# Patches of layer 2: the next exponential ahead of the root's steps, a function table loaded ahead of the first square, and one constant copied by ScalarE

## The chip, the cores and the metric

The kernel runs on one core of a Trainium2 chip. The time is device time in microseconds (us) of one execution. Ten executions of the kernel before took between 6381.21 and 6408.22 us, with a median of 6394.25 us. One more execution was taken with the hardware profiler: it took 6396.54 us, and its span, from its first to its last instruction, is 6394.8 us. All durations below are from that execution, and all times inside it are counted from the start of its span.

The engines of the core are called TensorE (PE in the profile, with PEld for its loads of weights), VectorE (DVE), ScalarE (ACT), GpSimd (POOL) and SyncE (SP, which here only issues transfers). Each engine works through its own list of instructions in order, and an instruction that waits holds up all that stand behind it on that engine.

## The reference: what is computed

The input is x of shape (4, 192, 64, 64): four images of 192 channels. Four layers follow one another: layer 0 (a deformable convolution, channel attention and an MLP), layer 1 (attention of all 4096 positions with all others), layer 2 (attention in overlapping windows, then a gate and an MLP) and layer 3 (a small convolution whose weights come from the mean of the image). The change lies in the attention of layer 2, and in one constant. What matters of the reference:

```python
y = _conv1x1(_ln_c(x, n1g, n1b), qkv_w, qkv_b)       # layer norm over channels, then q, k, v
cols = _unfold(y, WS, STRIDE, PAD)                   # 8x8 windows, 6 apart: 11 x 11 of them
...
attn = jnp.einsum('blhic,blhjc->blhij', q, k)
attn = attn + bias[None, None]
e = jnp.exp(attn - jnp.max(attn, axis=-1, keepdims=True))
s = jnp.sum(e, axis=-1, keepdims=True)
s_img = _reverse(s, H, W)                            # overlapping windows are added up
o = jnp.einsum('blhij,blhjc->blhic', e, v)
o_img = _reverse(o, H, W).reshape(B, HEADS, ch, H, W)
out = (o_img / s_img[:, :, None]).reshape(B, C, H, W)
```

`_ln_c` subtracts the mean over the channels and multiplies with `rsqrt(var + 1e-05)`.

## The kernel before, in words

The kernel takes the images one after the other. For each image b the layers run mostly one behind the other, and the attention of layer 2, here called the patches, is the function `windows(b, ...)` (line 1060). Most of the program is ordered by a scheduler. The main part of `windows` stands in a block `with tc.manual_schedule()` (line 1311): there the instructions of each engine keep the order in which the code issues them.

**The rows of windows.** The image has 11 rows of windows, `wr` = 0 to 10, with 11 windows each. A row is worked on in three groups `g` of four windows (three in the last group), and a group in two pairs. For one group:

- `scores(wr, g)`: TensorE multiplies q and k (line 1185) into the PSUM tile `s`, of which there is one; VectorE adds the bias (line 1191) and so makes the tile `ex`.
- `lowered` takes off the maximum (VectorE, lines 1201 and 1202), and ScalarE then takes the exponential of `ex` in place (line 1333 for the first group, 1368 for all others). It covers 128x768 elements.
- `summed` adds up the exponentials (VectorE, lines 1207 and 1211).
- `turned(wr, g, pair)`: TensorE computes v (line 1228) and transposes the exponentials (line 1236); ScalarE copies both out of PSUM (lines 1233 `vs`, and 1240 `et`).
- `outputs` multiplies them (TensorE, lines 1256 and 1264) for the pair before the one that was just turned.

The tiles of `v`, `t`, `qk` and `rb` share one PSUM tag `a` with two buffers, so that each of these products on TensorE needs the reader of the last but one to have ended.

The exponential is issued one group ahead: in group g the code issues the scores of the next group first, then both pairs of its own group, and at the end, behind the pairs, the exponential of the next group.

**The layer norm of later rows** is cut into steps (`norm_steps`, line 1107) that `links` advances up to a named point. For row wr + 2 the square (ScalarE, line 1112) is issued in group 0 of row wr, the sums over channels (TensorE, `variances`, line 383) and the inverse root at the end of group 1 (`norm(wr + 2, INVERSE)`, line 1365), and the spreading over partitions (TensorE, line 392, `pb`) in group 2. The steps of the root, called the root's steps here, are: a square of the mean (ScalarE, line 400), two operations of VectorE (lines 401 and 402), and then on ScalarE a logarithm (line 363) and an exponential (line 364). They stand ahead of the next group's exponential of line 1368.

**The sums of a row** are inverted in group 1 of the row after it, between its two pairs: `inverses` (line 1289) issues a logarithm (line 1295) and an exponential (line 1296) on ScalarE. In group 2, `finish` (line 1298) spreads them with TensorE (line 1301, `rb`), and VectorE multiplies (line 1302).

**The function tables.** ScalarE evaluates Ln, Exp, Gelu and others from a table set that must be loaded before; a load is an instruction of its own on ScalarE (`ACT_TABLE_LOAD` in the profile). The kernel issues some loads by hand with `table`; where an activation is not served by the set that the program's builder takes to be loaded, the builder puts a load right in front of it, and this load then carries the activation's line number.

```python
    def table(name):
        if in_order and in_order[0] != name:
            in_order[0] = name
            if name == GELU:
                nc.scalar.preload_act_table(AF.Gelu)        # line 356
            else:
                nc.scalar.preload_act_table_set(name)       # line 358

    def inverse_root(r, pv):
        table(LN_EXP)
        nc.scalar.activation(r, pv, AF.Ln, bias=eps)        # line 363
        nc.scalar.activation(r, r, AF.Exp, scale=-0.5)      # line 364
```

`LN_EXP` is the set that has both Ln and Exp. The list `in_order` remembers the set that was loaded last by hand; it is non-empty only inside the blocks with a manual order. In the patches it is appended, and `table(LN_EXP)` called, right behind the square of row 0 and two warming products; later calls from `inverse_root` find the name unchanged and issue nothing.

**Warming.** `keep_warm(p, n)` (line 748) issues n products of TensorE whose result nobody reads, to fill its idle time. At the head of the patches they write the tile `warm`.

**The constant.** `constants` (line 181) is a generator that prepares weights during layer 0 of the first image. One of its steps collects biases in the tile `wide` (128x46) from PSUM (lines 239 to 255), with a copy on VectorE at the end.

Of the kernel before, what the change touches and what calls it, by code (L numbers as in the profile page):

```python
# [12 lines left out]
AF = mybir.ActivationFunctionType  # L13
# [20 lines left out]
LN_EXP, GELU = "natural_log_exp_and_others", "gelu"  # L34
# [22 lines left out]
NWIN = 11  # L57
# [24 lines left out]
def conv_seq_kernel(ctx: ExitStack, tc: tile.TileContext, a, out: bass.AP):  # L82
    nc = tc.nc

    def pool_of(**kw):

        return tc.tile_pool(**({} if kw.get("space") == DRAM else {"reuse_waits": "tile"}), **kw)
# [7 lines left out]
    def const(shape, name):  # L95
        return wpool.tile(shape, F32, tag=name, name=name)
# [89 lines left out]
    def constants():  # L186
# [53 lines left out]
        with pool_of(name="wideps", bufs=1, space=PSUM) as pp:  # L240
            n = sum(n for name, n in _V96 if name in _WIDE)
            wide = const([M, 2, n], "wide")
            p = pp.tile([M, 2, n], F32, tag="p", name="p_wide")
            at = 0
            for name, n in _V96:
                if name in _WIDE:
                    cols = slice(at, at + n)
                    at += n
                    for to, of, k in (
                        (p[0:P, 0, cols], slice(0, P), 0), (p[P:M, 0, cols], slice(0, M - P), 1),  # L250
                        (p[0:Q, 1, cols], slice(M - P, P), 1), (p[Q:M, 1, cols], slice(M - P, P), 1),
                    ):
                        nc.tensor.matmul(to, lhsT=ident[:P, of], rhs=V[name][:, k, :], start=True, stop=True)
                    VW[name] = wide[:, :, cols]
            nc.vector.tensor_copy(wide, p)
        yield
        fc1_dram, fc1_bias = folded("fc1", V["l0_g2"], V["l0_b2"], V["l0_bfc1"])
        yield
# [2 lines left out]
        with pool_of(name="foldq", bufs=1, space=PSUM) as pp:  # L261
            p = pp.tile([128, 2, 512], F32, tag="p", name="p_qkv")
# [15 lines left out]
        with pool_of(name="outb", bufs=1, space=PSUM) as pp:  # L278
            p = pp.tile([P, 2], F32, tag="outb", name="pob")
# [69 lines left out]
    in_order = []  # L349
# [6 lines that stand above are left out]
                nc.scalar.preload_act_table(AF.Gelu)  # L356
            else:
                nc.scalar.preload_act_table_set(name)
# [76 lines left out]
    def links(steps, upto=None):  # L435

        while True:
            try:
                link = next(steps)
                if upto is not None and link == upto:  # L440
                    return None
            except StopIteration as end:
                return end.value
# [304 lines left out]
    def keep_warm(p, n):  # L748

        m, width = p.shape  # L750
        columns = spread.rearrange("p j n -> p (j n)")[:, 0:width]
        for _ in range(n):
            nc.tensor.matmul(p, lhsT=ident[:, 0:m], rhs=columns, start=True, stop=True)
# [306 lines left out]
    def windows(b, oi, load_image):  # L1060
# [3 lines left out]
        with ExitStack() as s:  # L1064
# [6 lines left out]
            def new_rows(wr):  # L1071

                top = STRIDE * wr - PAD
                r0, r1 = (PAD if wr == 0 else WS - STRIDE), min(WS, H - top)
                return r0, r1, top + r0
# [31 lines left out]
            def norm_steps(wr, src, dst, rows):  # L1107

                n, name = src.shape[2], f"l2n1_{b}_{wr}"
                q = n // 4  # L1110
                sq = s1.tile([P, 2, 512], F32, tag="ln_sq", name=f"sq_{name}", bufs=2)[:, :, :n]
                nc.scalar.activation(sq, src, AF.Square)
                yield SQUARE
                pv = ps.tile([128, 512], F32, tag="n", name=f"pv_{name}")
                variances(pv[:, 0:q], src, mean192)
                variances(pv[:, 128 : 128 + q], sq, mean192)
                r = s1.tile([128, 128], F32, tag="ln_r", name=f"r_{name}", bufs=2)[:, 0:q]
                spread_variance(r, pv[:, 0:q], pv[:, 128 : 128 + q])
                yield from inverse_root_steps(r, r)
                pb = spread_quarters(r, n, P, ps, name).rearrange("p (r c) -> p r c", r=rows)  # L1120
                for k in range(2):
                    nc.vector.tensor_tensor(dst[:, k], src[:, k, :].rearrange("p (r c) -> p r c", r=rows), pb, ALU.mult)

            def norm(wr, upto=None):

                r0, r1, _ = new_rows(wr)
                if wr not in norms:
                    norms[wr] = norm_steps(wr, given.pop(wr), sets[wr % 2][0][:P, :, r0:r1, inside], r1 - r0)
                links(norms[wr], upto)
# [180 lines left out]
            groups = -(-NWIN // WG)  # L1310
            with tc.manual_schedule():
                warm = ps2.tile([128, 512], F32, tag="a", name=f"warm_{b}")[:, 0:384]
                norm(0, SQUARE)
                keep_warm(warm, 2)
                in_order.append(None)
                table(LN_EXP)
                norm(0, VARIANCE)
                keep_warm(warm, 2)
                norm(0)
                keep_warm(warm, 1)  # L1320
                shared(0, 0)
                project_rows(0, 0)
                norm(1, SQUARE)
                project_rows(0, 1)
                norm(1, VARIANCE)
                queries(0)
                inputs(0)
                norm(1)
                shared(1, 0)
                load(2)  # L1330
                ex, top = scores(0, 0)
                lowered(0, 0, ex, top)
                nc.scalar.activation(ex, ex, AF.Exp)
                due = None
                for wr in range(NWIN):
                    for g in range(groups):
                        nxt = (wr, g + 1) if g + 1 < groups else (wr + 1, 0)
                        if 0 < wr < NWIN - 2 and g == 0:
                            norm(wr + 2, SQUARE)
                        if nxt[0] < NWIN:  # L1340
                            sc, top = scores(*nxt)
                        sums = summed(wr, g, ex)
                        if nxt[0] < NWIN:
                            lowered(*nxt, sc, top)
                        if wr + 3 < NWIN and g == 1:
                            load(wr + 3)
                        for pair in range(WG // 2):
                            ops = turned(wr, g, pair, (ex, sums))
                            if due is not None:
                                outputs(*due)  # L1350
                                if g == 0 and pair == 0:
                                    collect(wr - 1)
                            due = ops
                            if g == 0 and wr + 1 < NWIN:
                                project_rows(wr + 1, pair)
                            if wr == 0 and g == 0 and pair == 0:
                                norm(2, SQUARE)
                            if wr > 0 and g == 1 and pair == 0:
                                inverses(wr - 1)
                            if wr > 0 and g == 2:  # L1360
                                finish(wr - 1, pair)
                            if wr + 2 < NWIN and g == 2 and pair == 0:
                                norm(wr + 2)
                        if wr + 2 < NWIN and g == 1:
                            norm(wr + 2, INVERSE)
                        if nxt[0] < NWIN:
                            ex = sc
                            nc.scalar.activation(ex, ex, AF.Exp)
                        if g == 0 and wr + 1 < NWIN:
                            for i in (1, 2):  # L1370
                                shared(wr + 1, i)
                            queries(wr + 1)
                            inputs(wr + 1)
                        if g == 2 and wr + 2 < NWIN:
                            shared(wr + 2, 0)
                    if wr == 1:
                        load_image()
                outputs(*due)
                collect(NWIN - 1)
                inverses(NWIN - 1)  # L1380
                keep_warm(ps2.tile([128, 512], F32, tag="a", name=f"warm2_{b}")[:, 0:384], 4)
                for h in range(2):
                    finish(NWIN - 1, h)
                in_order.pop()
# [611 lines left out]
    with ExitStack() as s:  # L1996
        sb, pool = (s.enter_context(pool_of(name=n, bufs=1)) for n in ("norms0", "l0d0"))
        ps = s.enter_context(pool_of(name="l0dps", bufs=2, space=PSUM))
        wide = s.enter_context(pool_of(name="l0dps2", bufs=5, space=PSUM))
# [119 lines left out]
```

## Time and profile before

| what | value |
|---|---|
| time, median of 10 (lowest, highest) | 6394.25 us (6381.21, 6408.22) |
| time of the profiled execution | 6396.54 us |
| its span | 6394.8 us, 106283 instructions |
| PE / PEld busy | 5921.8 us (93%) / 4052.4 us (63%) |
| DVE / ACT / POOL busy | 4603.1 (72%) / 3778.3 (59%) / 2107.3 us (33%) |
| TensorE's granted clock, mean | 0.961 |
| table loads on ScalarE, all lines | 164, of 1283 ns each |
| the patches of the four images | about 1481 to 1752, 2997 to 3268, 4514 to 4786, 5755 to 6025 us |

A row of busy time sums an engine's instructions. TensorE's products are pipelined and their ends are modelled, so that 93% doesn't mean that it runs at its peak. A line of the timeline gives the start, the time until the end, the engine, the source line, the operation, out<-in, how many instructions were merged, and in brackets how long the engine stood idle just before and who ended that. A line of a stretch (windows) gives start and end, the length, the busy time of each engine with its count of instructions, TensorE's granted clock as a share of full speed, and the share and rate of the DMA engines.

### The profile page before, as it was taken

The numbers are of one execution on the slowest core, as the hardware profiler recorded it, in microseconds if no ns is written. First come the engines' busy times: TensorE is split into PE (matmuls) and PEld (weight loads), VectorE is DVE, ScalarE is ACT, GpSimd is POOL, SyncE is SP. The second block draws the span as 40 slices with busy tenths as digits, with TensorE's granted clock in tenths as the row PEclk, the third lists the DMA queues.
The fourth block names the chain that finished last, engine by engine and source line by source line (L and its number), as shares of the span: only waits on it lengthen the run. The fifth ranks groups of instructions, "written<-read, shape, count | busy, mean of one in ns | idle before, by whom it ended". The sixth has DMA issues, their size and how long they took to land.

```text
span 6394.8 us, 106283 instructions
## 1 busy us (share of the span) xinstructions
PE 5921.8 (93%) x40528; PEld 4052.4 (63%) x40528; DVE 4603.1 (72%) x6850; ACT 3778.3 (59%) x6552; POOL 2107.3 (33%) x2293
## 2 busy tenths in 40 slices
PE   7888999999989899999988899999998989999897
PEld 4555688886644568887654458888654457776543
DVE  3764199985578669996676839998567867765667
ACT  3764388875654358885654438887565436545542
POOL 2763077752200037772210008775220000003200
PEclk8889999999989899999998999999998999999998
DMA  6995267751010266772110057775101020001000
GB/s 191 300 314 159 85 193 224 224 180 37 24 29 16 73 197 218 229 225 72 34 35 25 20 138 229 223 224 171 38 24 29 18 62 11 13 15 36 7 7 22
DMA packets 330116, 698.59 MB, mean 109 GB/s; under 512 B 59894, under 2 KB 216838, under 8 KB 328839
## 3 DMA queue, kind: packets, MB, share of 16 engines
q0 software_dynamic: 92736, 455.22, 21.7%
q1 hardware_dynamic: 236038, 235.78, 13.4%
q8 instruction: 321, 5.26, 0.3%
q14 instruction: 189, 1.54, 0.1%
q10 hardware_dynamic: 832, 0.79, 0.0%
HBM read 611.25 MB, written 78.87 MB: 108 GB/s over the span
## 4 chain that ended last, share of the span: by engine, by line
PE 65%; DVE 18%; ACT 7%; DMA 5%; issue 4%; POOL 1%; SPq 0%; DVEq 0%; ACTq 0%; POOLq 0%
PE y L1041 11%; PE s L973 10%; PE h L650 7%; DMA ring<-table,idx 2%; PE po L538 2%; PE v L1228 2%; DVE ha L1412 2%; PE h L1604 2%; PE qk L1150 2%; PE o L878 2%; PE qk L1151 2%; DVE ga L1412 2%; DVE gate L1412 2%; DVE row L639 1%; PE t L1236 1%
## 5 line engine op out<-in xcount | busy, mean ns | idle before, releaser
L632 POOL DMA_INDIRECT ring<-table,idx x1152 | 1673.5, 1453 | 949.8 <-DMA wkT<-in_wkT_dram 269.8
L973 PE MATMUL s<-ths,ph 96*128 96x256 f32 x4096 | 981.9, 381 | 5.1 <-ACT sc L975 2.8
L973 PEld LDWEIGHTS s<-ths,ph 96*128 96x128 f32 x4096 | 776.4, 191 | 129.0 <-ACT sc L975 4.5
L638 ACT ACTIVATE row<-ring,pos 128x384 f32<-128x384 f32 x1152 | 672.7, 609 | 235.0 <-DVE xo L643 146.1
L639 DVE SCALAR_TENSOR_TENSOR row<-ring,fr,row 128x384 f32<-128x384 f32 x1152 | 675.6, 615 | 109.1 <-ACT row L638 103.7
L1041 PE MATMUL y<-sc,gx 128*97 128x256 f32 x3008 | 716.4, 379 | 0.0
L1041 PEld LDWEIGHTS y<-sc,gx 128*97 128x97 f32 x3008 | 489.3, 164 | 127.6 <-issue 5.1
L642 ACT ACTIVATE xo<-row,pos 128x192 f32<-128x192 f32 x1152 | 486.0, 448 | 70.3 <-PE h L650 33.7
L643 DVE SCALAR_TENSOR_TENSOR xo<-row,fr,xo 128x192 f32<-128x192 f32 x1152 | 446.8, 413 | 38.7 <-ACT xo L642 36.8
L975 ACT COPY sc<-s 128x1024 f32<-128x1024 f32 x376 | 377.4, 1004 | 156.8 <-PE s L973 153.5
L1038 DVE TENSOR_TENSOR sc<-sc,mbs 128x1024 f32<-128x1024 f32 x376 | 453.7, 1219 | 19.9 <-ACT mbs L999 19.9
L1039 ACT ACTIVATE sc<-sc 128x1024 f32<-128x1024 f32 x376 | 393.3, 1053 | 75.1 <-DVE sc L1038 71.9
L980 DVE TENSOR_TENSOR top<-top,sc 128x1024 f32<-128x1024 f32 x282 | 344.5, 1222 | 127.2 <-ACT sc L975 127.0
L650 PE MATMUL h<-ti,xo 128*128 128x192 f32 x2304 | 434.6, 327 | 0.0
L650 PEld LDWEIGHTS h<-ti,xo 128*128 128x128 f32 x2304 | 388.8, 190 | 28.8 <-issue 8.6
L650 PE MATMUL h<-kept,xo 128*128 128x192 f32 x960 | 243.5, 386 | 66.8 <-DVE xo L643 58.9
L1412 DVE SCALAR_TENSOR_TENSOR ga<-gate,v,ga 128x1024 f32<-128x1024 f32 x234 | 300.4, 1284 | 6.7
L1654 POOL COPY gate<-gate 128x192 f32<-128x192 f32 x12 | 4.2, 349 | 903.9 <-ACT gate L1647 903.9
L1191 DVE TENSOR_TENSOR ex<-s,bias 128x768 f32<-128x768 f32 x132 | 126.1, 956 | 242.2 <-PE s L1185 238.7
L650 PEld LDWEIGHTS h<-kept,xo 128*128 128x128 f32 x960 | 173.2, 213 | 160.9 <-DVE xo L643 116.8
L855 PE MATMUL h<-d_l0m,fc 128*128 128x256 f32 x768 | 215.5, 424 | 59.1 <-ACT z L1610 22.5
L1240 ACT COPY et<-t 64x384 f32<-64x384 f32 x484 | 232.0, 479 | 58.1 <-PE t L1236 51.9
(403 smaller groups left out, 11136.6 us busy)
## 6 DMA issues: line engine op xcount, KB each, us to landing
ti<-table SPq DMA_DIRECT2D x768, 48.0 KB
ring<-table,idx POOLq DMA_INDIRECT x1152, 5.1
xnd<-xn SPq DMA_DIRECT2D x4, 3270.0 KB
xi<-in_x_dram SPq DMA_DIRECT2D x32, 384.0 KB
xk<-xd SPq DMA_DIRECT2D x32, 384.0 KB
xd<-xc SPq DMA_DIRECT2D x64, 192.0 KB
table<-tt SPq DMA_DIRECT2D x32, 384.0 KB
xc<-xd SPq DMA_DIRECT2D x60, 192.0 KB
```

Of the source, the lines that this page charges most:

```text
L632: nc.gpsimd.indirect_dma_start(out=gt.rearrange("p q r c -> p (q r c)"), out_offset=None, in_=corners, in_offset=bass.IndirectOffsetOnAxis ...
L638: nc.scalar.activation(row, gt[:, 0], AF.Copy, scale=pos[:, t, 9 + tap : 10 + tap])
L639: nc.vector.scalar_tensor_tensor(row, gt[:, 1], fr[:, t, 9 + tap : 10 + tap], row, ALU.mult, ALU.add)
L642: nc.scalar.activation(xo[:, j, :], row[:, 0, :], AF.Copy, scale=pos[:, t, tap : tap + 1])
L643: nc.vector.scalar_tensor_tensor(xo[:, j, :], row[:, 1, :], fr[:, t, tap : tap + 1], xo[:, j, :], ALU.mult, ALU.add)
L650: nc.tensor.matmul(acc[m // 2][:, bass.ts(m % 2, C)], lhsT=xo.rearrange("p j c -> p (j c)")[:, bass.ts(m, 128)], rhs=tt, start=t == 0 and ...
L973: nc.tensor.matmul(p[:, t, :], lhsT=ph[:, bass.ts(G * g + t, 128)], rhs=ths[i], start=True, stop=True)
L975: nc.scalar.copy(to, p)
L1038: nc.vector.tensor_tensor(ex, ex, mbs[i].unsqueeze(1).to_broadcast([128, G, QN]), ALU.add)
L1039: nc.scalar.activation(ex, ex, AF.Exp)
L1041: nc.tensor.matmul(py, lhsT=gx[:, G * g + t, :], rhs=ex[:, t, :], start=g == 0 and t == 0, stop=g == NG - 1 and t == G - 1,)
L1412: nc.vector.scalar_tensor_tensor(acc[:, b], src(tap, b), w[:, tap : tap + 1], acc[:, b], ALU.mult, ALU.add)
```

## The change

Three edits, in the functions `constants` and `windows`:

1. The copy of the constant `wide` out of PSUM goes from VectorE to ScalarE.
2. At the head of the patches, `in_order.append(None)` and `table(LN_EXP)` move ahead of the square of row 0, and six more warming products are issued between them and the square.
3. Inside the rows, the exponential of the next group moves from the end of the group to its second pair, right behind that pair's `turned` and `outputs`. It so comes ahead of the projections of the next row's second half in group 0, ahead of the root's steps in group 1, and ahead of `finish` in group 2.

```diff
-            nc.vector.tensor_copy(wide, p)
+            nc.scalar.copy(wide, p)
...
                 warm = ps2.tile([128, 512], F32, tag="a", name=f"warm_{b}")[:, 0:384]
+                in_order.append(None)
+                table(LN_EXP)
+                keep_warm(warm, 6)
                 norm(0, SQUARE)
                 keep_warm(warm, 2)
-                in_order.append(None)
-                table(LN_EXP)
                 norm(0, VARIANCE)
...
                             due = ops
+                            if pair == 1 and nxt[0] < NWIN:
+                                ex = sc
+                                nc.scalar.activation(ex, ex, AF.Exp)
                             if g == 0 and wr + 1 < NWIN:
                                 project_rows(wr + 1, pair)
...
                             norm(wr + 2, INVERSE)
-                        if nxt[0] < NWIN:
-                            ex = sc
-                            nc.scalar.activation(ex, ex, AF.Exp)
                         if g == 0 and wr + 1 < NWIN:
```

## The prediction, made before the changed kernel was run

> **What bounds the kernel now.** I read the page first: the span, the busy shares, and the chain that ended last by engine.
>
> ```profile
> span 6394.8 us, 106283 instructions
> PE 5921.8 (93%) x40528; PEld 4052.4 (63%) x40528; DVE 4603.1 (72%) x6850; ACT 3778.3 (59%) x6552; POOL 2107.3 (33%) x2293
> PE 65%; DVE 18%; ACT 7%; DMA 5%; issue 4%; POOL 1%; SPq 0%; DVEq 0%; ACTq 0%; POOLq 0%
> ```
>
> TensorE carries the chain, ScalarE has 7% of it. But the change touches one stage, so the second view is busy time in the stretches of the four patches.
>
> ```profile
> 1481.00:1752.00 271.00, 250.92 (x3776) 165.02 (x3774) 158.78 (x235) 166.46 (x354) 76.58 (x207) 0.97 0.12 30
> sum 1084.00, PE 1001.72 PEld 659.10 DVE 635.32 ACT 665.46 POOL 312.49; mean PE 250.43 PEld 164.78 DVE 158.83 ACT 166.36 POOL 78.12
> ```
>
> 1084 of 6395 us are patches, and ScalarE is busy for 61% of them. That looks like room, so the third view is its timeline around one place: row 6, from group 1 into group 2.
>
> ```profile
> 1629.25 0.97 ACT L1240 COPY et<-t 64x384 f32<-64x384 f32 x2
> 1630.25 0.52 ACT L1295 ACTIVATE rs<-ot 6x384 f32<-6x384 f32 x1
> 1630.80 0.52 ACT L1296 ACTIVATE rs<-rs 6x384 f32<-6x384 f32 x1
> 1631.35 0.32 ACT L1233 COPY vs<-v 128x192 f32<-128x192 f32 x1
> 1631.56 0.97 ACT L1240 COPY et<-t 64x384 f32<-64x384 f32 x2
> 1632.55 0.25 ACT L400 ACTIVATE r_l2n<-pv_l2n 128x96 f32<-128x96 f32 x1
> 1633.38 0.37 ACT L363 ACTIVATE r_l2n<-r_l2n,eps 128x96 f32<-128x96 f32 x1 [0.57 <-DVE r_l2n L402]
> 1633.78 0.28 ACT L364 ACTIVATE r_l2n<-r_l2n 128x96 f32<-128x96 f32 x1
> 1633.97 0.83 ACT L1368 ACTIVATE ex<-ex 128x768 f32<-128x768 f32 x1
> 1634.70 0.30 ACT L1233 COPY vs<-v 128x192 f32<-128x192 f32 x1
> ```
>
> For 5.5 us ScalarE has no gap but the 0.57 us in which VectorE works on the root. TensorE's timeline shows who needs it:
>
> ```profile
> 1634.85 0.55 PE L1236 MATMUL t<-ident,ex 128*128 128x128 f32 x3 [1.24 <-ACT ex L1368]
> 1635.84 0.89 PE L1301 MATMUL rb<-rs,headsel 128*96 128x384 f32 x2
> ```
>
> The transposes wait 1.24 us for the exponential, and `rb` cannot start before `vs` (1635.0) has freed its PSUM buffer. So once a row, of 22.9 us (from the `et` at 1606.3 to that at 1629.25), ScalarE sets the pace, just where its two logarithms and their exponentials stand.
>
> **What the change does to the instructions.** I compared the order of instructions on each engine in the two built kernels. VectorE loses the copy of `wide`, TensorE gains 6 warming products an image, POOL and SyncE keep their order, DMA issues and queues included. On ScalarE the exponentials move as the diff says. But it has 343 table loads instead of 164. The hand-issued load, now first in its block and with no input, is placed at the top of the whole program: eight loads stand there, Ln-and-Exp and Gelu in turn, where one stood. When the patches come, layer 1 has left another set loaded, and the builder puts a load before every Ln and the Exp behind it:
>
> ```
> L1295 load; L1295 Ln; L1296 load; L1296 Exp; ... L363 load; L363 Ln; L364 load; L364 Exp
> ```
>
> These are 44 at each of the four lines, 176 in all; with three more at the top, 179. The list of before can be trusted here: its 164 loads are, line by line, those in the trace (41+37+24+23+20+4+4+4+4+3). The exponentials of 128x768 need none, since an Exp always ran last.
>
> A load costs this:
>
> ```profile
> 12.41 1.28 ACT L372 ACT_TABLE_LOAD   x1 [1.25 <-PE pv_l L383]
> 13.70 0.37 ACT L372 ACTIVATE r_l<-pv_l,eps 128x128 f32<-128x128 f32 x1
> 1769.35 1.28 ACT L372 ACT_TABLE_LOAD   x1
> 1771.06 0.40 ACT L372 ACTIVATE r_l0m<-r_l0m,eps 128x128 f32<-128x128 f32 x1 [0.43 <-DVE r_l0m L402]
> ```
>
> 1.28 us, and the activation starts 0.01 later. The second pair has the form of line 363: the load runs at once and the activation alone waits for VectorE, so the load covers that wait.
>
> Two statements of the Trainium skill are set against these rows. "ScalarE: Activation LUTs", What ACT_TABLE_LOAD costs, adds a drain of about 1380 ns to each switch; the 0.01 us above shows none, and with it 176 loads would cost 243 us more. Its Table sets section says that Ln followed by Exp needs one load, since one set has both; by that the 176 loads would not exist and the time would hardly change. The built order shows them.
>
> **The cost, step by step** (one image).
>
> *Rows 1 to 8.* I replay the timeline above with the new order, durations and steps unchanged. `et` ends at 1630.22; load to 1631.52; Ln to 1632.06; load to 1633.35; Exp to 1633.88; `vs` and `et` of the second pair take 1.18 as before, to 1635.09; now the exponential, to 1635.95 (the next can start at 1635.85); the square of the mean to 1636.12; load, which covers the 0.57, to 1637.4; Ln to 1637.8; load to 1639.1; Exp to 1639.4; `vs` to 1639.7; `rb` at 1639.75, not 1635.84. That is 3.9 us a row. The bounds: 5.13 if none of the four loads were covered, 2.5 if two of them fell into waits. The move itself, which was to take away the 1.24 us, gains nothing at `rb`: `vs` still stands behind the root's steps. In groups 0 and 2 it only fills gaps of ScalarE (0.88 us idle before `qs` at 1625.98). 8 x 3.9 = 31.2.
>
> *Row 0* has no sums to invert: only `pb` waits for the root. The exponential and two loads come ahead of it; 1522.28 becomes about 1523.2: 0.9. *Rows 9 and 10* and the end have no root but the two loads of `inverses`: 2.5 each, 7.5. In row 10 TensorE waits 0.82 us for that chain already, so none is covered.
>
> *The head.* For row 0's norm ScalarE waits 1.16 us for VectorE, which hides most of the first load: 0.15 + 1.28 = 1.4. For row 1's, 0.73 + 1.28 = 2.0: TensorE waits 1.63 us for it today. The old load there (1482.2) lay beside TensorE's work, its removal gains nothing. Of the six warming products two come between the last two products `wy` of layer 1, four behind them and straight ahead of the sums of row 0. One takes 0.78 us (the two behind the sums fill 1487.3 to 1488.9; each is two records). The two between the `wy` run from 1485.3 to 1486.9, partly in the 0.57 for which TensorE waits there now, and put the last `wy` (1486.0) off by 0.9; with the four behind it, 0.9 + 3.1 = 4.0. In the last image the scheduler puts them at the start of layer 1: one where TensorE waits 0.42 for a transfer, four ahead of `th` in an unbroken run of TensorE, one in a wait of 0.56: 0.4 + 3.1 = 3.5.
>
> Sum: 31.2 + 0.9 + 7.5 + 3.4 = 43.0, times four 172; warming 3 x 4.0 + 3.5 = 15.5; together 187.5.
>
> *Top of the program.* Eight loads take 10.3 us from 0.73 on, to 11.0; the first square starts at 10.1 today: 0.9. *The copy of `wide`*: 0.21 us on VectorE, for which TensorE waits 0.31; ScalarE is idle from 105.6 to 121.4. Between 0.2 gained and 0.2 lost; 0. All this gives 188.
>
> *TensorE's clock.* The waits grow long, and the clock follows idleness:
>
> ```profile
> 1584.49:1587.90 3.41, 2.17 (x62) 1.64 (x64) 1.94 (x4) 2.34 (x7) 0.00 (x0) 1.00 0.00 0
> 1587.90:1591.32 3.42, 3.42 (x26) 2.33 (x24) 2.90 (x5) 0.96 (x2) 0.00 (x0) 0.50 0.00 0
> ```
>
> The granted clock changes on a grid of 3.41 us. Here 2.17 busy us in one such window gave half clock in the next. Counted over the whole trace, 48 of the 50 full-clock windows that were busy at most 52% were followed by half clock, and one of the 1590 that were busy above 72%. In the replay TensorE has nothing from 1632.7 to 1639.75 but `v` (0.8), `t` (0.5) and `o` (0.5): a whole window always lies inside these 7.05 us and is at most 53% busy, so each of these rows should lose the full clock. A half-clock window of 3.41 us costs 1.7 where TensorE works through it, and often it takes two (3.4): I take 2.5 a row. Below, nothing if the windows stay above the limit; above, 5, as in the 10.2 us spells at each head now. 8 x 2.5 + 4 for head, last rows and end = 24, times four: 96.
>
> 188 + 96 = 284. On the profiled execution's 6396.54 us that is **6680 us**; it lies 2 us above the median of the runs, so the forecast holds for either.
>
> **The rivals.**
>
> *A. Loads and clock*, as above: 6680, between 6630 and 6735. **0.74**.
>
> *B. Loads, but the clock holds*, since the grid splits the idle stretch luckily or `v` and `t` stretch over it: 6396.5 + 188 = 6585, 6560 to 6610. For it: two windows with 64% busy, from 1632 and from 1656, kept full clock. Against: those had 1.7 us idle, not 5. **0.16**.
>
> *C. The loads cost nothing* on the chip, because a load of a set with both functions is found in place; then only the move and the warming count. Price: at most the 1.24 us of each of 9 rows of 4 images, 45 us, against 15.5 of warming, so 6367; at least nothing, as `vs` stays behind the root, so 6412. I take 6390, the middle. It decides from the point where a load costs under about 0.1 us. Against: all 164 loads in the trace, also those of a set loaded shortly before, take 1283 ns. **0.04**: 0.02 faster, 0.02 within.
>
> *D. Each load drags more than its duration*, or half clock spreads over whole rows: from 5 us a row of clock and 5.1 of loads, 36 rows: 6396.5 + 364 + 16 = 6776, and up to 6850. **0.06**.
>
> **The numbers.** A and B lie both above 6396; the range takes in all of A and the upper part of B: 6570 to 6735. This kernel's measurement can tell about 0.2% from no change. Slower by more: A, B, D, 0.96; faster 0.02; the same 0.02.
>
> **What would show it.** In the profile after: loads at lines 363, 364, 1295 and 1296, 44 each, of 1283 ns; `rb` in group 2 waiting for ScalarE by 3 to 4 us; the four patches near 340 us each instead of 271; granted clock in them near 0.87 instead of 0.97; everything outside them unchanged to within some us. Loads missing from the trace would make it C; patches of 320 us at a clock of 0.97, B; transposes that still wait for the exponential longer than `rb` waits, a fault in the replay.

## The result, and the profile after

The changed kernel takes 6722.8 us, the median of eight runs (6716.69 to 6731.89); the kernel before, run beside it, 6397.84 us. The ratio is 1.0507, with a 95% interval of 1.0496 to 1.0519. So it is slower by 5%, and 43 us above the forecast. The ratios here and below leave out two executions of one kernel (no_hoist), which took 8535 and 7231 us at a granted clock of 0.65 and 0.79.

First the page: span, busy time of each engine and the chain that ended last.

```profile
span 6726.5 us, 106522 instructions
PE 6106.5 (91%) x40576; PEld 4156.9 (62%) x40576; DVE 4605.1 (68%) x6849; ACT 4012.0 (60%) x6732; POOL 2098.9 (31%) x2293
PE 64%; DVE 16%; ACT 10%; DMA 5%; issue 3%; SPq 1%; POOL 0%; DVEq 0%; ACTq 0%; POOLq 0%
```

The span is 331.7 us longer. ScalarE has 180 more instructions (the 179 loads and the copy of `wide`) and 234 us more of work; 179 x 1.283 is 230. Its share of the chain rises from 7% to 10%. The groups of ScalarE by line show the loads (count, busy us and mean ns of one, idle time before):

```profile
L363 ACT ACT_TABLE_LOAD x44 | 56.5, 1283 | 0.8
L364 ACT ACT_TABLE_LOAD x44 | 56.5, 1283 | 0.8
L1295 ACT ACT_TABLE_LOAD x44 | 56.5, 1283 | 0.8
L1296 ACT ACT_TABLE_LOAD x44 | 56.5, 1283 | 0.8
...
L356 ACT ACT_TABLE_LOAD x40 | 51.3, 1283 | 0.7
```

These are the counts of the built order: 44 at each of four lines, and three more at line 356 (40 instead of 37). Next the patches of the first image as one stretch:

```profile
1488.00:1838.00 350.00, 294.69 (x3787) 188.66 (x3786) 159.52 (x235) 222.38 (x397) 76.70 (x207) 0.81 0.09 24
```

350 us where there were 271, VectorE and POOL unchanged, ScalarE 56 us more. TensorE is busy for 44 us more although it has only 11 more records in the stretch: its granted clock is 0.81 instead of 0.97. From the first square to the last multiplication of line 1302, the patches take 349.6, 349.5, 349.7 and 349.3 us, and took 270.6, 270.7, 270.8 and 269.4: 316.4 of the 331.7 us. The stretch up to the first square is 0.9 us longer at its start, as the loads at the top begin everything later; the other 14 us lie in the layers outside the patches. There the two programs differ only in the copy of `wide` and in the last image's six warming products, which stand at the start of its layer 1. The time up to the last product `y` of layer 1 (line 1041) in the first image alone differs by over 13 us among before, after and the runs of the first two sets below (1481.1 to 1494.6 us).

Now the place that the prediction replayed, on ScalarE (start, duration, line, out<-in), some rows later:

```profile
1674.67 0.97 ACT L1240 COPY et<-t 64x384 f32<-64x384 f32 x2
1675.66 1.28 ACT L1295 ACT_TABLE_LOAD   x1
1676.95 0.52 ACT L1295 ACTIVATE rs<-ot 6x384 f32<-6x384 f32 x1
...
1683.36 1.28 ACT L364 ACT_TABLE_LOAD   x1
1684.65 0.28 ACT L364 ACTIVATE r_l2n<-r_l2n 128x96 f32<-128x96 f32 x1
1684.84 0.30 ACT L1233 COPY vs<-v 128x192 f32<-128x192 f32 x1
```

and the waits of TensorE there (in brackets, with the releaser):

```profile
1679.70 0.93 PE L1228 MATMUL v<-qkvT,xw 96*128 96x192 f32 x4 [1.52 <-ACT vs L1233]
1681.43 0.90 PE L1236 MATMUL t<-ident,ex 128*128 128x128 f32 x3 [0.80 <-ACT ex L1357]
1685.19 1.59 PE L1301 MATMUL rb<-rs,headsel 128*96 128x384 f32 x2 [1.96 <-ACT vs L1233]
```

`rb` starts 10.52 us after the start of `et`; before it was 6.59 (1635.84 - 1629.25), and the replay had 10.50 (1639.75 - 1629.25). The delay of 3.9 us is spread over three waits, and part of it is filled because TensorE works slower. The row after row period is 30.6 to 30.7 us instead of 22.96, 7.7 more. The loads explain 3.9 of it.

### The profile page after: what moved, and what is told of

Same layout as the page of the kernel before. It is cut to its first block, busy times and chain, and to the rows that moved or that the text cites. A ratio compares the mean times of both kernels' runs of the same rounds, so it can differ in the third digit from the quotient of the medians.

```text
span 6726.5 us, 106522 instructions
## 1 busy us (share of the span) xinstructions
PE 6106.5 (91%) x40576; PEld 4156.9 (62%) x40576; DVE 4605.1 (68%) x6849; ACT 4012.0 (60%) x6732; POOL 2098.9 (31%) x2293
## 4 chain that ended last, share of the span: by engine, by line
PE 64%; DVE 16%; ACT 10%; DMA 5%; issue 3%; SPq 1%; POOL 0%; DVEq 0%; ACTq 0%; POOLq 0%
PE y L1041 11%; PE s L973 10%; PE h L650 6%; PE v L1228 2%; PE qk L1150 2%; DVE ha L1413 2%; PE h L1605 2%; DMA ring<-table,idx 2%; PE o L878 2%; PE qk L1151 2%; PE rb L1301 2%; DVE ga L1413 2%; PE po L538 2%; DVE gate L1413 1%; PE h L855 1%
## 5 line engine op out<-in xcount | busy, mean ns | idle before, releaser
L1228 PE MATMUL v<-qkvT,xw 96*128 96x192 f32 (+3 forms) x1056 | 270.3, 384 | 67.0 <-ACT vs L1233 67.0
L1280 POOL TENSOR_TENSOR ot<-ot,ot 102x128 f32<-102x128 f32 x80 | 59.0, 739 | 803.5 <-ACT ot L1274 781.7
```

The costliest lines, as they stand in the source:

```text
L1228: nc.tensor.matmul(pv, lhsT=xw[: P + k, k, both, :].rearrange("p w j -> p (w j)"), rhs=qkvT[: P + k, k, 2 * C :], start=k == 0, stop=k == 1,)
```

## The experiments

The theory: the time is lost by the 176 loads in the patches, half directly on ScalarE and half by the clock that TensorE loses in the waits. The rivals: the moved exponential or the warming products cost the time; a load ahead of the square is bad where it stands, whatever it does to the others; the loads alone cost all of it, and the clock is only a companion. Ten kernels were run, in three sets. Ratios are to the kernel before, run beside each set (6400.44 us for the first four kernels, 6406.3 for the next four). "Patches" is the time per image from the first square to the last multiplication, "row" the steady period in rows 3 to 8.

| kernel | loads | time, us | ratio (95% interval) | patches, us | row, us |
|---|---|---|---|---|---|
| before | 164 | 6397.84 | 1 | 269.4-270.8 | 22.96 (some 24.5) |
| after | 343 | 6722.8 | 1.0507 (1.0496-1.0519) | 349.3-349.7 | 30.6-30.7 |
| no_hoist | 164 | 6382.25 | 0.9965 (0.9953-0.9978) | 264.6-266.8 | 22.31 |
| table_alone | 343 | 6700.77 | 1.0473 (1.0455-1.0490) | 342.6-347.2 | 29.0-31.8 |
| move_alone | 164 | 6364.88 | 0.9948 (0.9933-0.9962) | 260.3-262.1 | 22.31 |
| warm_alone | 164 | 6413.67 | 1.0025 (1.0012-1.0038) | 3.1 more in three heads | 22.96 |
| warm_rows | 343 | 6624.92 | 1.0347 (1.0315-1.0378) | 318.1-329.3 | 26.4 or 27.3 |
| loads_g1 | 324 | 6701.44 | 1.0463 (1.0433-1.0494) | 343.5-345.0 | 30.6-30.7 |
| loads_g0 | 324 | 6675.19 | 1.0425 (1.0395-1.0454) | 336.9-338.8 | 29.3-30.5 |
| move_inv | 164 | 6342.58 | 0.9897 (0.9875-0.9920) | 256.2-258.9 | 21.71 |
| held | 164 | 6550.19 | 0.9975 (0.9956-0.9994) | 261.2-268.2 | 22.31 |
| held_inv | 164 | 6505.76 | 0.9910 (0.9887-0.9932) | 254.9-256.4 | 21.73 |

The last two were run where the kernel before took 6564.24 us, on another chip (the last `y` of the first image's layer 1 ends at 1609 us in held and 1591 us in held_inv), so only their ratios and their patches can be set against the others.

**Which part of the change.** The four kernels of the first set each undo one part of the change or do one alone. no_hoist is the changed kernel with the load put back behind the square:

```diff
-                in_order.append(None)
-                table(LN_EXP)
                 keep_warm(warm, 6)
                 norm(0, SQUARE)
                 keep_warm(warm, 2)
+                in_order.append(None)
+                table(LN_EXP)
```

> The changed kernel with the table load put back behind row 0's square; the copy by ScalarE, the six warming products and the earlier exponential stay. Theory H (the 179 added loads make the loss, and the load's place at the head makes the loads): 164 loads again, patches near 271 us plus 4 for the warming at each head, granted clock in them 0.97, time within 15 us of before, 6385 to 6420. Rival E (the earlier exponential or the warming makes the loss): 6600 or more. Rival H' (the loads make about 190 us and something else the rest): 6480 to 6560.

Measured: 0.9965. The loads of lines 363, 364, 1295 and 1296 are gone, and with them the whole loss, and more: the time is 3 us under the expected 6385 to 6420. Its patches as a stretch:

```profile
1482.07:1748.84 266.77, 250.47 (x3787) 165.87 (x3786) 158.08 (x235) 167.12 (x354) 76.79 (x207) 0.98 0.11 31
```

ScalarE's 55 us and TensorE's 44 us of the changed kernel are both gone with the loads, and the clock is back at 0.98. Two lines of the program ahead of or behind a square thus make 5%.

table_alone is the kernel before with only those two lines moved ahead of the square.

```diff
+                in_order.append(None)
+                table(LN_EXP)
                 norm(0, SQUARE)
                 keep_warm(warm, 2)
-                in_order.append(None)
-                table(LN_EXP)
```

> The kernel before with only the table load ahead of the square (no warming, old place of the exponential). Theory H: 343 loads and patches as long as after or longer, since in the old order both the logarithms and their loads stand ahead of the exponential that TensorE waits for: 6700 to 6770; the earlier exponential then won back part of the loss. Rival E: near 6400. Rival H'': below 6650, if the earlier exponential is part of the loss.

Measured: 1.0473, so nearly all of the 5.07% by itself. The expectation also had the earlier exponential win back part of the loss in the changed kernel; that isn't seen, as the changed kernel is 22 us slower than this one.

move_alone is the kernel before with only the exponential moved (the third edit of the change).

> The kernel before with only the exponential moved to the second pair. Theory H with the step of the prediction that the move gains nothing at rb: between 0 and 3 us an image, 6385 to 6400, the wait of 1.24 us for the exponential gone and a wait of about the same length for vs at rb in its place. Rival M (the move takes the wait of 1.24 us away in 36 rows): 6350 to 6360. Rival E: slower by over 1%.

Measured: 0.9948. The move alone is a gain, of 7.3 to 10.5 us an image, 0.65 in each row. This contradicts the prediction's step that it gains nothing at `rb`. TensorE's timeline, same place:

```profile
1636.04 0.92 PE L1228 MATMUL v<-qkvT,xw 96*128 96x192 f32 x4
1636.80 0.55 PE L1236 MATMUL t<-ident,ex 128*128 128x128 f32 x3
1638.54 0.89 PE L1301 MATMUL rb<-rs,headsel 128*96 128x384 f32 x2 [0.68 <-ACT vs L1233]
```

`t` follows `v` without a wait, and `rb` now waits 0.68 for `vs`. It starts 5.94 us after the `et` (1632.60), not 6.59. Besides, the rows of 24.5 us, which had a half-clock window in them, are nearly gone.

warm_alone is the kernel before with only the six products.

```diff
+                keep_warm(warm, 6)
                 norm(0, SQUARE)
                 keep_warm(warm, 2)
```

> The kernel before with only the six warming products ahead of row 0's square. By the prediction's step 4.0 us at each of three heads and 3.5 us in the last image, 15.5 in all: 6405 to 6418. Rival W (the products only fill idle time, or win the cost back by keeping the clock up at the head): 6390 to 6400.

Measured: 1.0025, 13 us. From the square to the sums it takes 8.24 us instead of 5.17 in three heads, and 5.08 as before in the fourth.

**The clock's share.** warm_rows is the changed kernel with four more products whose result nobody reads in each of rows 1 to 8, where TensorE waits in group 2. They add 3.1 us of work a row (0.78 each) and change no table load.

```diff
+                        if 0 < wr < NWIN - 2 and g == 2:
+                            keep_warm(ps.tile([128, 3, 512], F32, tag="s", name=f"fill1_{b}_{wr}")[:, 0, 0:384], 2)
                         if nxt[0] < NWIN:
                             sc, top = scores(*nxt)
...
+                            if 0 < wr < NWIN - 2 and g == 2 and pair == 0:
+                                keep_warm(ps.tile([128, 3, 512], F32, tag="s", name=f"fill2_{b}_{wr}")[:, 0, 0:384], 2)
                             if wr > 0 and g == 2:
                                 finish(wr - 1, pair)
```

> The changed kernel, loads and all, with four warming products in each of rows 1 to 8: two ahead of the next row's first scores and two ahead of rb, in TensorE's idle time of about 5 us at that place. They are 3.1 us of more work for TensorE a row, and nobody reads them. Theory T (of the 7.7 us that a row is longer, about half is the half clock that follows the idle time): granted clock of the patches from 0.81 back to 0.95 or more, rows at 26.5 to 27.5 instead of 30.66, time 6580 to 6630. Rival L (the loads alone make the 7.7 us, through ScalarE): clock up, rows unchanged, time 6720 or, with the added work, up to 6800.

Measured: 1.0347, 98 us less than the changed kernel, for more work. The grid of the clock shows why. First the changed kernel, five stretches of 3.41 us from the start of group 2's wait (start and end, length, busy time of PE, PEld, DVE, ACT, POOL with counts, granted clock, DMA share and rate):

```profile
1677.06:1680.48 3.42, 1.90 (x71) 1.46 (x61) 0.27 (x1) 3.36 (x6) 0.00 (x0) 1.00 0.00 0
1680.48:1683.89 3.41, 1.95 (x20) 1.07 (x19) 2.17 (x4) 3.31 (x6) 0.00 (x0) 0.50 0.02 5
1683.89:1687.30 3.41, 2.11 (x7) 1.39 (x8) 2.43 (x5) 2.09 (x5) 0.00 (x0) 0.50 0.00 0
1687.30:1690.72 3.42, 3.02 (x12) 1.77 (x11) 1.16 (x3) 0.31 (x1) 0.00 (x0) 0.50 0.11 18
1690.72:1694.13 3.41, 3.41 (x67) 1.90 (x66) 0.55 (x1) 1.95 (x3) 0.00 (x0) 0.50 0.19 68
```

then warm_rows in the same group of a row:

```profile
1658.18:1661.59 3.41, 2.07 (x24) 1.23 (x23) 2.02 (x4) 3.31 (x6) 0.00 (x0) 1.00 0.00 0
1661.59:1665.01 3.42, 2.89 (x16) 1.69 (x15) 3.09 (x6) 2.25 (x5) 0.00 (x0) 1.00 0.00 0
```

In the changed kernel a window that is 56% busy (1.90 of 3.42) is followed by four windows at half clock; 88% busy (3.02) in one of them does not bring the full clock back; after the next one, busy throughout, the window from 1694.13 has it again. In warm_rows the emptiest window shown is 61% busy (2.07) and the clock holds. Its first and third image keep the full clock in nearly all rows, with a row of 26.4 us. In the second and fourth, the emptiest window of each of the rows 3 to 8 is 60 to 62% busy and is followed by one window at half clock, and the row takes 27.3 us: 0.9 more for the same instructions. So the expected clock of 0.95 in the patches was reached in the third image only (0.94, 0.90, 0.95, 0.89). By the rows of 26.4 the clock costs 30.7 - 26.4 = 4.3 us a row, or more if the added products are in the way, and the loads, with what the products cost, 26.43 - 22.96 = 3.5. The rival by which the loads cost all of it falls: some half of the loss in these rows is the clock's.

**Where the loads stand.** Two kernels have the kernel before with 160 loads issued by hand, four in each of rows 1 to 10: loads_g1 ahead of the inverses in group 1, loads_g0 in group 0 behind the second projections (there the first condition of the diff reads `g == 0 and pair == 1`).

```diff
+                            if wr > 0 and g == 1 and pair == 0:
+                                for _ in range(2):
+                                    nc.scalar.preload_act_table(AF.Gelu)
+                                    nc.scalar.preload_act_table_set(LN_EXP)
                             if wr > 0 and g == 1 and pair == 0:
                                 inverses(wr - 1)
```

> The kernel before with four table loads more in each of rows 1 to 10, issued by hand in group 1 right ahead of the logarithm of the sums, 160 in all; the exponential in its old place, the first load behind the square. They take the place of the builder's loads and nothing else is changed. Theory T: each costs its 1.28 us in full there, as no wait covers it, 5.1 us a row, and the clock falls as in the changed kernel: rows of 30 to 32 us, time 6690 to 6750. Rival K (the changed kernel's loss needs the moved exponential or the head): below 6500.

> The same four loads a row, but in group 0 behind the projections of the second pair, where ScalarE has gaps of 0.7 to 0.9 us at each copy. Theory G (as the prediction reads group 0: gaps that can be filled): they cost no more than 2 to 3 us a row, time 6480 to 6530. Rival S (ScalarE and TensorE hand two PSUM buffers to and fro, so that in no group is there room for a load and the place makes no difference): rows of 30 to 32 us, within 30 us of the kernel with the loads in group 1.

Measured: 1.0463 and 1.0425. In group 0 they cost nearly as much as in group 1, though ScalarE's 61% of busy time had left room for them on paper. TensorE's timeline of loads_g0 in group 0:

```profile
1643.05 0.90 PE L1236 MATMUL t<-ident,ex 128*128 128x128 f32 x3 [5.01 <-ACT ex L1372]
```

The transposes now wait 5.01 us for the exponential that stands behind the loads, nearly their whole 4 x 1.283 = 5.13 us. The idle time of ScalarE in these groups is in small pieces, and neither of the two places tried has room for 5 us. In both kernels the exponential has its old place, behind the loads; loads behind a moved exponential, or in group 2, were not tried.

**What the move leaves.** In move_alone, `rb` still waits for ScalarE. move_inv is move_alone with the inverses taken out of group 1.

```diff
-                            if wr > 0 and g == 1 and pair == 0:
+                            if wr > 0 and g == 0 and pair == 1:
                                 inverses(wr - 1)
```

> The kernel before with the exponential moved as in the change, the first load behind the square, no warming, and the inversion of the sums moved from group 1 to group 0 of its row, behind the projections of the second pair. If ScalarE's work between the two pairs of group 1 holds TensorE up (1.1 us a row), this gains 0.5 to 0.7 us a row more than the moved exponential alone, 18 to 28 us: 6335 to 6350. Rival: group 0 has no room either, then within 8 us of the moved exponential alone, 6357 to 6373.

Measured: 0.9897, with a row of 21.71 us; 64 us faster than the kernel before. The wait of TensorE that paced group 2, over some four rows (1640 to 1740 us; us in total, times, longest), was in before

```profile
PE t L1236 <- ACT ex L1368: 4.3, 4, 1.3
```

and in its place move_alone has the first line, and move_inv the second:

```profile
PE rb L1301 <- ACT vs L1233: 2.0, 3, 0.7
PE rb L1301 <- ACT vs L1233: 0.2, 1, 0.2
```

What is left of the transposes' waits for ScalarE is the 0.4 us a row that before has too. So two activations of 0.52 fit into group 0, where four loads of 1.28 did not.

**Is it the place or the hoisting?** held is the changed kernel with an anchor: a copy of one column of row 0's input, on ScalarE, ahead of the load. In the built order the load then stays where the text of the program has it.

```diff
+                first = s1.tile([P, 1], F32, tag="first", name=f"first_{b}")
+                nc.scalar.copy(first, given[0][:, 0, 0:1])
                 in_order.append(None)
                 table(LN_EXP)
                 keep_warm(warm, 6)
```

> The changed kernel with one more instruction on ScalarE at the head of each image's patches: a copy of one column of row 0's input (128x1), ahead of the hand-issued load. In the built order the load then keeps its place, straight ahead of the square, where the diff's text puts it, and 164 loads are left. Theory L (the loss comes from the 179 loads that the hoisting brings, and not from where the load of the patches stands): like the version with the load behind the square, 6370 to 6395 us, patches near 265 us an image, rows of 22.3 us, granted clock in the patches 0.96 or more. Rival P (a load ahead of the square does harm by itself, since the square and the sums behind it come later): above 6450 us, with the time lost at the head, square to sums over 10 us.

Measured: a ratio of 0.9975, with 164 loads, against no_hoist's 0.9965, the intervals overlapping. The times are above the 6370 to 6395 expected, since all times were 2.6% higher there; by the ratio the expectation is met. The head is no longer either: from the last product `y` of layer 1 to the sums of row 0, 1.80 + 6.74 = 8.54 us, and 0.30 + 8.24 = 8.54 in no_hoist. So a load ahead of the square is harmless in itself; what it lost by was that, with nothing to hold it, it went to the top of the program.

held_inv is move_inv with the same anchor and the load ahead of the square, without warming products.

> The kernel before with the exponential moved, the inverses of the sums moved to the second pair of group 0, and the load held ahead of the square by the same one-column copy; no warming products. 164 loads. Theory L with the step of the prediction that the old load at the head lay beside TensorE's work: nothing gained by it, 6330 to 6355 us, within 10 us of the version without it (6342.6), the head's square to sums between 4.5 and 5.5 us. Rival Q (taking the load off the root's way at the head gains its 1.28 us and the clock window behind it, four times): 6320 to 6330 us.

Measured: 0.991, as move_inv's 0.9897. From the last `y` of layer 1 to the sums, the head takes 1.80 + 3.68 = 5.48 us as in move_inv (0.30 + 5.18). From that product to the end of the patches, the four images take 1029 us in sum, in move_inv 1030. So the earlier load gains nothing, and the rival's 10 us and more are not there. The expectation of 4.5 to 5.5 us for square to sums was missed (3.68), because the copy and the load now take their 1.5 us ahead of the square.

## Why the prediction was right, and where it was off

The sign, the cause and the range were right; the forecast of 6680 us was 43 us low, and the result lies 12 us under the upper end of the range. By its own steps:

- **The extra loads**: right, 44 at each of four lines, 1283 ns each, and eight at the top, where the first square starts at 11.04 us instead of 10.10: 0.9, as predicted. no_hoist, table_alone and held show that they come from the hoisting, and carry nearly all of the loss.
- **The replay of a row**: right, `rb` 10.52 us after the `et`, predicted 10.50. It expected `rb` to wait 3 to 4 us; the waits of `v`, `t` and `rb` are 1.52, 0.80 and 1.96, 4.3 together. The exponential still ends the wait of `t`, but for less time than `rb` waits, so that the named fault of the replay did not occur.
- **"The move itself ... gains nothing at `rb`"**: wrong for the move by itself. The step compared the end of `vs`, which indeed stays, and left out that on TensorE `t` and `o` stand between the wait for the exponential and `rb`. In the kernel before they ran after that wait; moved, they run ahead of the wait for `vs`: 6.59 becomes 5.94 us, and 35 us in all (move_alone). In the changed kernel this gain can't be seen: it is 13 us of warming and 9 us more above table_alone; why was not tried.
- **"In groups 0 and 2 it only fills gaps"**: too sure. loads_g0 shows that ScalarE has no room in group 0 for 5 us; that 0.84 of an exponential fits is what move_alone shows.
- **TensorE's clock**: right in kind, and the term that was mis-sized. 2.5 us a row were taken; the steady row lost 7.7 - 3.9 = 3.8 by the replay, and 4.3 or more by warm_rows. The step counted one or two half-clock windows a row; in the steady rows there are four. It did not ask what brings the full clock back. In the whole trace of after, none of the 121 half-clock windows that were busy under 80% was followed by full clock, 8 of 43 between 80 and 90%, and 85 of 112 at 98% or more: mostly it takes a window without idle time, and at times even that is not enough. So the signs it named were missed too: 349.5 us for the patches instead of 340, and a clock of 0.81 instead of 0.87. Per image, with the replay's 43.0 for the loads and 2.3 for the warming taken off the 79.1 by which the patches grew (316.4 / 4), 33.8 are left, where 24 were predicted; that is 39 us of four images. The clock's loss is spread over the patches: in the first image (32.9 left) rows 1 to 8 grew by 56.1 together, 7.0 a row, as some rows of before have half-clock windows and the first rows of after are shorter. Less 31.2 for the loads this leaves 24.9, 3.1 a row, where 20 were predicted; the other 8 lie in the head, in row 0 and in rows 9 and 10 (the next two points), where 4 were predicted.
- **Rows 9, 10, row 0 and the end**: the end costs 2.5 as predicted. Rows 9 and 10 cost 4.1 and 4.3 instead of 2.5, and the way from the first scores to the end of row 0 4.6 instead of 0.9. Whether it is the clock there wasn't tried by itself.
- **The head**: warming 3.06 instead of 4.0. The two products between the `wy` put the last `wy` off by 0.56 (from 4.57 to 5.13 us behind the square) instead of 0.9, and the four behind it put the sums off by another 2.5 instead of 3.1; by the median of warm_alone 13 us in all (predicted 15.5). From the sums to the first scores 4.35 instead of 3.4.
- **The copy of `wide`**: nothing was seen, and it had no run of its own. no_hoist stands at 6382, move_alone plus warming at 6364.9 + 13 = 6378; that leaves no room for more than a few us.

Rival B, 6585 with the clock held, is what warm_rows comes near to where it holds it (6625 with 3.1 us of extra work a row). Of rival D's two conditions, loads that drag more than their duration did not occur: `rb` is late by 3.93 us and not 5.1. Its half clock over whole rows did in part, 39 of the 104 windows of the first image's patches against 5 of 81.

Two statements of the Trainium skill stand beside these rows. "ScalarE: Activation LUTs", section What ACT_TABLE_LOAD costs, adds a drain of about 1380 ns; in the rows of after the activation follows its load at 0.01 us (1675.66 + 1.28, and 1676.95), and by that figure 176 drains would have made an estimated 243 us more. "TensorE: Matmul & The Clock Gate", section Why this matters for your kernels, asks for no idle gap over about 3 us to keep the clock. In the three waits shown none is longer than 2.0 us, and the clock goes. What goes with the loss here is the busy share of a window of the grid: in the trace of after, 96 of the 103 full-clock windows that were busy at most 56% were followed by half clock, and 3 of the 1550 above 62%.

## What to carry to other kernels

Compare the built order of instructions before costing an edit: an instruction without inputs is held only by what stands ahead of it in its block, and a table load that loses this neighbour may turn up elsewhere and bring loads at every later use. A change is best judged part by part: here one part gained 0.5%, another cost 0.25%, and a third, which on paper moved one load past a square and two products, cost 4.7%. When an engine that paces TensorE gets later, price the wait twice, once for itself and once for the clock in the windows after it, and allow for several windows at half clock: here four followed the waits of each steady row.

## What the runs showed of the hardware that was not expected

- In the changed kernel and in loads_g1 the rows approach a period of 30.70 to 30.72 us and stay there, whatever row they start from (28.2, 30.59, 30.61, 30.67, 30.69, 30.70 in the first image of after). Nine windows of the clock's grid are 9 x 3.413 = 30.72 us. The rows so fall in step with the grid, the same four windows being half each time. The rows of 27.3 us in warm_rows, with one half-clock window each, are eight windows (27.31). Cause and effect were not tried apart.
- Four table loads a row cost nearly the same in two places of the row (1.0463 and 1.0425) and as inserted ones (table_alone, 1.0473).
- A small gain in a wait also paid at the clock: the rows of some 24.5 us, seven of the 28 in rows 2 to 8 of before, are missing from move_alone and move_inv, although the move takes only 0.65 us off a row.
